# Stretches of the edge softmax shifted by half a stretch in a four-layer graph network

## The chip, the cores and the metric

The kernel runs on one core of one Trainium2 chip. A core has five engines with a queue of instructions each: TensorE (PE; its loads of weights are listed apart, as PEld), VectorE (DVE), ScalarE (ACT), GpSimd (POOL) and SyncE (SP), which here only issues DMAs. The metric is the device time of one execution in microseconds (us). The time before is 3351.46 us, the median of three runs (3344.36 to 3361.28).

## The reference, cut to what matters

A graph has 3125 nodes with 256 values each and 50000 edges, sorted by their target `dst`. Four layers follow one another, each as `x = layernorm(x + layer(x))`. Layer 0 is a gated message passing layer and layer 3 a relational one (a weighted sum over incoming edges, then block-diagonal products); the change touches neither. Layers 1 and 2 both need a softmax over the incoming edges of every node, for each head:

```python
# layer 1: 4 heads, 8 relations, 4 node types
score = sum(q_att[etype, dst] * k[src], axis=-1) * (relation_pri[etype] / sqrt(64))
m     = segment_max(score, dst)
ex    = exp(score - m[dst])
agg   = segment_sum(ex / segment_sum(ex, dst)[dst] * msg[etype, src], dst)
# layer 2: 8 heads of 64
e     = s_src[src] + s_tgt[dst];  e = where(e >= 0, e, 0.2 * e)
ex    = exp(e - segment_max(e, dst)[dst])
out   = elu(segment_sum(h[src] * ex / segment_sum(ex, dst)[dst], dst) @ Wo + bo)
```

All of it is float32; the edges are drawn so that some nodes have very many incoming edges (`dst` is 3125 times the square of a uniform number).

## The kernel before, in words

**Tiles, groups, stretches.** Nodes are kept in 25 tiles of 128. Edges are put into 416 *slot tiles* (`TT`) of 128 places each; a slot tile belongs to one node tile, so that sums over its edges are one matmul with a one-hot matrix (place to node). Four slot tiles are a *group* (`G`), of which there are 104, and sixteen are a *stretch* (`S`), of which there are 26. All this is worked out on the chip from `dst` during the set-up (`bucket`, line 213). A part of it, `segments` (line 360), makes for every slot tile five rows of 128 numbers, `seg`, which say where a node's run of edges starts and ends (0 or a large negative number `NEG`), and for the whole list three rows of one number per slot tile, `astart`, `aend` and `anew` (does a run reach from one tile into the next), from which `rows` is made, one row of two times sixteen per stretch. `seg` is stored by SyncE at line 403, the three rows are copied by VectorE at line 405, `rows` is put together at lines 407 to 410 and stored at 411.

**The softmax layers.** Layer 1 (line 1105) and layer 2 (line 1374) both call `edge_softmax` (line 714) with a function `score` of their own. `score` works on one group: GpSimd gathers the group's 512 rows from a table in memory with four indirect DMAs (line 509; a row is 2 KB in layer 1 and a little over that in layer 2), into one of seven buffers; SyncE loads the group's one-hots, two groups at a time (`onehots_back`, line 541; the DMA is at line 548); and then

- in layer 1 (line 1228) PE selects the targets' vectors (`pqe`, line 1237), VectorE multiplies them with the gathered rows (`pd`, line 1242) and sums over each head (`sc`, line 1243);
- in layer 2 (line 1390) PE selects the targets' scores (`pst`, line 1398) and three small VectorE instructions add the gathered ones and apply the slope (`pl`, `sc`, lines 1403 to 1405).

After the four groups of a stretch comes `softmax` (line 607) for its sixteen slot tiles at once. It is one chain that goes to and fro between engines: SyncE loads the stretch's rows of `seg` (line 615) and `rows` (line 619); PE transposes the scores so that each (head, tile) pair is a row (line 624); VectorE adds the mask (`smA`, line 627), runs a maximum scan forward and one backward along the row (`smf`, `smb`, lines 629 and 631); PE moves the last elements of the rows to one partition (lines 633, 634); VectorE and ScalarE scan over the sixteen tiles there and hand a running maximum on to the next stretch (`hand`, `smo`, lines 638 to 652); the result goes back (`cc`, line 649), VectorE takes it in (`smb`, line 660), subtracts (`smA`, line 661), PE transposes back (line 664) and ScalarE takes the exponential (`ex`, line 666). If the stretch isn't the first, the maximum of the node whose run goes on from the stretch before may have grown; then the sums of that node tile so far are multiplied with a factor (`dif` line 669, `fac` line 676, product at line 679).

`weigh` (line 682) then takes one group of an earlier stretch: ScalarE makes the one-hots float32 (line 693); VectorE multiplies some heads of the gathered rows with `ex` (line 697) and ScalarE the others (lines 694 and 701), which gives `r`; for every slot tile PE multiplies the one-hot with `r` (line 706) and VectorE adds the product to the node tile's sums in `acc` (line 711). A gather buffer is free for the next group when `r` is made.

**The order.** `edge_softmax` goes through the stretches. In each it scores group n of this stretch and then weighs group n of the stretch before, for the first three groups; the fourth group of the stretch before is weighed step by step between the steps of the softmax of this one. So the first stretch has nothing to weigh, and after the last one its four groups are weighed alone. Once the sums are whole, the layer divides by the summed weights (`rd`, line 1263 in layer 1, line 1419 in layer 2). With seven buffers the gathers of seven groups may be under way before the first group is weighed.

At the end of layer 1 the node tiles' outputs are turned into layer 2's table (`nodes2`, line 1316, and its weights' work at lines 1336 and 1337). Layer 2 needs its input x back in order of nodes: `x_back` (line 1357, the DMAs in `back`, line 1371) is kept on a list and issued from `edge_softmax` (line 726) when its third iteration begins. In what order the instructions stand in an engine's queue is set by the scheduler of the language's tile framework, from the order of the program and what each instruction needs; it may differ from the order of the program's text.

## Time and profile before

One execution under the profiler is shown; its time is 3366.77 us, its span 3365.0 us.

| what | before |
|---|---|
| median of three runs | 3351.46 us (3344.36 to 3361.28) |
| the profiled execution: time, span | 3366.77 us, 3365.0 us |
| mean granted clock of TensorE | 0.845 of full speed |
| PE, its weight loads, VectorE, ScalarE, GpSimd busy | 80, 52, 67, 43, 54% of the span |
| DMA | 658.40 MB, 196 GB/s over the span |
| layer 1, from the first `smA` (line 627) to `rd` (line 1263) | 1197.66 to 1811.01: 613.4 us |
| layer 2, from the first `smA` to `rd` (line 1419) | 1994.48 to 2672.97: 678.5 us |

How it is read: a busy share is that of an engine over the whole span; the page also gives it in 40 slices of 84.1 us each, as a digit of tenths. A line of the timeline has the start of an instruction in us from the span's start, its duration, its engine, its line in the kernel, the operation, what it writes and what it reads, with partitions x elements, and in brackets how long the engine was idle before it and what ended that. SPq and POOLq are the queues that issue DMAs.

### The profile page before, as it was taken

What the parts mean: (1) busy time and instruction counts of PE and PEld (TensorE: products, weight loads), DVE (VectorE), ACT (ScalarE), POOL (GpSimd) and SP (SyncE); (2) the same over time, 40 slices, a digit from 0 to 9 for tenths busy, and PEclk for the clock granted to TensorE, in tenths of its full rate; (3) what the DMA queues carried; (4) which work ended last, traced back from release to release, by engine and by line L of the source; (5) the groups of instructions that cost most, each with busy time, mean ns of one, the idle gap of its engine ahead of it and who ended that gap; (6) DMA issues with size and microseconds to landing.
All of it is one profiled execution on the core that took longest, in us unless ns stands there. A gap on an engine that the chain in (4) does not pass through costs nothing. (4 is left out here: it accounts for less than half of the span.)

```text
span 3365.0 us, 50575 instructions
## 1 busy us (share of the span) xinstructions
PE 2690.9 (80%) x12679; PEld 1750.5 (52%) x12679; DVE 2267.3 (67%) x6030; ACT 1460.9 (43%) x4405; POOL 1832.7 (54%) x1850
## 2 busy tenths in 40 slices
PE   2779999999979767777775847888888886888885
PEld 1357777775546345555553525666666664333333
DVE  2546676667655479888886437888888873555555
ACT  1427777774456334545543215656656553000001
POOL 3037777771044166666661556766766202777773
PEclk9889999999989878888887968888888886656566
DMA  7249998894067877777774367877877235333333
GB/s 164 74 134 296 298 289 290 288 287 141 32 248 285 313 224 241 231 235 233 231 232 132 123 209 200 227 226 223 228 223 225 78 125 221 106 106 105 105 106 92
DMA packets 240632, 658.40 MB, mean 196 GB/s; under 512 B 47976, under 2 KB 87028, under 8 KB 234029
## 3 DMA queue, kind: packets, MB, share of 16 engines
q0 software_dynamic: 132400, 484.37, 46.9%
q1 hardware_dynamic: 104278, 167.53, 15.2%
q10 hardware_dynamic: 3676, 3.23, 0.5%
q8 instruction: 122, 2.00, 0.2%
q14 instruction: 156, 1.28, 0.1%
HBM read 513.06 MB, written 151.58 MB: 198 GB/s over the span
## 5 line engine op out<-in xcount | busy, mean ns | idle before, releaser
L509 POOL DMA_INDIRECT gb<-table,s_src x832 | 859.1, 1033 | 371.6 <-issue 201.2
L706 PE MATMUL pr<-r,oh 128*128 128x260 f32 x2496 | 735.8, 441 | 82.2 <-DVE acc L711 32.6
L706 PEld LDWEIGHTS pr<-r,oh 128*128 128x128 f32 x2496 | 503.2, 217 | 219.5 <-issue 37.2
L1509 POOL DMA_INDIRECT ring<-table,b_rel x391 | 369.7, 946 | 317.9 <-DVE oh L1519 199.1
L701 ACT ACTIVATE r<-gb,ex 128x64 f32<-128x64 f32 x2080 | 522.3, 335 | 0.0
L509 POOL DMA_INDIRECT gb<-table,s_rel x416 | 404.4, 972 | 205.8 <-issue 110.0
L711 DVE TENSOR_TENSOR acc<-acc,pr 128x260 f32 (+1 forms) x832 | 457.9, 550 | 73.0 <-PE pr L706 59.4
L1538 PE MATMUL pa<-ring,oh 128*128 x832 | 420.5, 617 | 92.3 <-DMA ring<-table,b_rel 44.6
L1538 PEld LDWEIGHTS pa<-ring,oh 128*128 128x128 f32 x832 | 190.7, 278 | 322.4 <-DVE oh L1519 210.8
L1545 DVE TENSOR_TENSOR x<-x,pa 128x256 f32 x416 | 175.2, 421 | 227.8 <-PE pa L1538 225.6
L1237 PE MATMUL pqe<-q_all,oht 128*128 x1248 | 207.1, 304 | 94.6 <-DVE pd L1242 78.7
L693 ACT CAST oh<-ohb 128x512 f32<-128x512 bf16 x208 | 128.3, 618 | 314.2 <-PE pr L706 284.3
L589 ACT ACTIVATE r<-mv,eps 128x4 f32<-128x4 f32 (+2 forms) x31 | 9.1, 295 | 527.8 <-DVE mv L575 524.4
L697 DVE TENSOR_TENSOR r<-gb,ex 128x512 f32<-128x512 f32 (+1 forms) x208 | 225.7, 1086 | 13.3 <-ACT ex L666 9.0
L979 PE MATMUL pa<-gb,ohw 128*128 128x272 f32 x832 | 223.4, 402 | 4.5 <-DVE acc L981 2.9
L1237 PEld LDWEIGHTS <-oht 128*128 128x128 bf16 x1248 | 130.6, 106 | 128.4 <-issue 87.6
L961 PE MATMUL pre<-xb,oht 128*128 x1248 | 193.7, 273 | 0.0
L981 DVE TENSOR_TENSOR acc<-acc,pa 128x272 f32 x416 | 179.7, 432 | 5.1 <-PE pa L979 2.8
L928 DVE TENSOR_TENSOR places<-iota,s_dl 128x512 bf16<-128x512 f32 x104 | 71.9, 691 | 160.8 <-ACT ohw L976 160.8
L956 PE MATMUL pre<-gb,idb 128*128 128x512 bf16 x624 | 169.3, 380 | 5.3 <-DMA gb<-table,s_src 5.3
L967 DVE SCALAR_TENSOR_TENSOR hg<-hg,aw 128x256 f32<-128x256 f32 x416 | 159.3, 420 | 16.4 <-ACT hg L965 16.4
L979 PEld LDWEIGHTS pa<-gb,ohw 128*128 128x128 f32 x832 | 141.2, 190 | 54.6 <-issue 34.0
(383 smaller groups left out, 4302.0 us busy)
## 6 DMA issues: line engine op xcount, KB each, us to landing
ohb<-oh_d SPq DMA_DIRECT2D x104, 256.0 KB
oht<-oht_d SPq DMA_DIRECT2D x104, 256.0 KB
table<-row SPq DMA_DIRECT2D x25, 1024.0 KB
gb<-table,s_src POOLq DMA_INDIRECT x832, 4.5
oh_d<-places SPq DMA_DIRECT2D x52, 256.0 KB
oht_d<-oht SPq DMA_DIRECT2D x52, 256.0 KB
sgm<-seg SPq DMA_DIRECT2D x26, 320.0 KB
gb<-table,s_rel POOLq DMA_INDIRECT x416, 4.7
```

The source lines that it names most:

```text
L509: self.nc.gpsimd.indirect_dma_start(out=out, out_offset=None, in_=table, in_offset=bass.IndirectOffsetOnAxis(ap=idx[:, t:t + 1], axis=0))
L697: nc.vector.tensor_mul(r[:, :, :nd, :hw], v[:, :, :nd, :], ex[:, :nd, s0:s0 + G].rearrange("p h t -> p t h")[:, :, :, None].to_broadcast([ ...
L701: nc.scalar.activation(r[:, j, h, :hw], v[:, j, h, :], AF.Copy, scale=ex[:, h, s0 + j:s0 + j + 1])
L706: nc.tensor.matmul(pr[:, n, :HB * F], oh[:, j, :], r[:, j, n * HB:(n + 1) * HB, :].rearrange("p h f -> p (h f)"), start=True, stop=True)
L711: self.used(nc.vector, nc.vector.tensor_add(a, a, pr[:, :, :HB * F]))
L961: last = nc.tensor.matmul(q, oht[:, 0, j, :], xbr[:, ds(node * (3 * D) + n * D, D)], start=False, stop=False)
L979: nc.tensor.matmul(pa, ohw[:, j, :], gb[:, j, 0:ET + D], start=True, stop=True)
L981: self.used(nc.vector, nc.vector.tensor_add(a, a, pa))
L1237: last = nc.tensor.matmul(pq[:, j, :], oht[:, j, :], q_all[:, ds(node * (3 * D) + n * D, D)], start=n == 0, stop=n == 2)
L1509: st = nc.gpsimd.indirect_dma_start(out=ring[:, at:at + D], out_offset=None, in_=table, in_offset=bass.IndirectOffsetOnAxis(ap=b_rel[:, b: ...
L1538: last = nc.tensor.matmul(pa, oh[:, j, :], ring[:, ds(at, D)], start=True, stop=True)
L1545: self.used(nc.vector, nc.vector.tensor_add(a, a, pa))
```

## The change

The slot tiles keep their order and their groups. What moves is where a stretch begins: all stretches are shifted by eight slot tiles (half a stretch, `L = S // 2`). There are 27 instead of 26. The first holds eight empty places and then the groups g0 and g1; the 25 after it hold four groups each; the last holds the groups g102 and g103 and eight empty places. For an empty place no group is scored, gathered or weighed. Its scores are set to 0 (a `memset` of `sc` in the first and the last stretch), its rows of `seg` are filled so that it is masked, and `astart`, `aend`, `anew` and `rows` are longer by sixteen places. The softmax of the two short stretches has the same instructions with the same shapes as the others.

```diff
         self.s_dl = c.tile([P, TT], F32, name="s_dl")
         self.s_ty = self.early.tile([P, TT], F32, name="s_ty")
         self.s_w = c.tile([P, TT], F32, name="s_w")
-        NS = TT // S
+        NS = TT // S + 1
         self.NB = -(-E // P)
...
-        self.seg = self.dram.tile([TT, 5, P], F32, name="seg")
+        self.seg = self.dram.tile([TT + S, 5, P], F32, name="seg")
         self.rows = self.dram.tile([NS, 2, S], F32, name="rows")
-        self.astart, self.aend, self.anew = (c.tile([1, TT], F32, name=n) for n in ("astart", "aend", "anew"))
+        self.astart, self.aend, self.anew = (c.tile([1, TT + S], F32, name=n) for n in ("astart", "aend", "anew"))
         self.tnode = c.tile([1, TT], I32, name="tnode")
         with tc.tile_pool(name="bk", bufs=1, side="right") as b:
...
     def segments(self, w, bd, nxt, prv, bdf, sel, kd):
         tc, nc, TT = self.tc, self.nc, self.TT
-        C = bd.shape[1]
+        C, L = bd.shape[1], S // 2
         flag = w.tile([P, 2, C, P], F32, name="flag")
         nc.vector.tensor_tensor(flag[:, 0], prv, bd, op=ALU.not_equal)
         nc.vector.tensor_tensor(flag[:, 1], nxt, bd, op=ALU.not_equal)
...
                 nc.vector.tensor_add(edge[:M], sg[:M, 0, 0:1], sg[:M, 1, 0:1])
                 for n, col in enumerate((sg[:M, 3, P - 1:P], sg[:M, 4, 0:1], edge[:M])):
                     nc.tensor.matmul(rows[:, n, m0:m0 + M], col, self.ident[:M, :M], start=True, stop=True)
-                nc.sync.dma_start(self.seg[m0:m0 + M], sg[:M])
+                M0 = M
+                if m0 + M == TT:
+                    assert M % 32 == 0 and M < P
+                    nc.vector.memset(sg[M:M + L, 0], NEG)
+                    nc.vector.memset(sg[M:M + L, 1:], 0.0)
+                    nc.sync.dma_start(self.seg[0:L], sg[M:M + L])
+                    M0 = M + L
+                nc.sync.dma_start(self.seg[L + m0:L + m0 + M0], sg[:M0])
             for n, row in enumerate((self.astart, self.aend, self.anew)):
-                nc.vector.tensor_copy(row, rows[:, n, :TT])
-            rrow = w.tile([1, TT // S, 2, S], F32, name="rrow")
+                nc.vector.memset(row, NEG if n == 2 else 0.0)
+                nc.vector.tensor_copy(row[:, L:L + TT], rows[:, n, :TT])
+            rrow = w.tile([1, TT // S + 1, 2, S], F32, name="rrow")
             nc.vector.memset(rrow, NEG)
             st, en = (r.rearrange("p (s t) -> p s t", t=S) for r in (self.astart, self.aend))
             nc.vector.tensor_copy(rrow[:, :, 0, 1:], st[:, :, :S - 1])
...
         nc = self.nc
-        R = H * S
+        R, p0 = H * S, t0 + S // 2
         sg = w.tile([R, 5, P], F32, name="sgm")
-        nc.sync.dma_start(sg, bass.AP(tensor=self.seg.tensor, offset=self.seg.offset + t0 * 5 * P,
+        nc.sync.dma_start(sg, bass.AP(tensor=self.seg.tensor, offset=self.seg.offset + p0 * 5 * P,
                                       ap=[[0, H], [5 * P, S], [1, 5 * P]]))
-        s_of = t0 // S
+        s_of = p0 // S
         rr = w.tile([1, 2, H, S], F32, name="rr")
         nc.sync.dma_start(rr, bass.AP(tensor=self.rows.tensor, offset=self.rows.offset + s_of * 2 * S,
                                       ap=[[0, 1], [S, 2], [0, H], [1, S]]))
...
         ends = sm.tile([1, 2, H], F32, name="ends")
         nc.vector.scalar_tensor_tensor(hand[(s_of + 1) % 2][:, 0, :, 0], o[:, 0, :, S - 1],
-                                       self.astart[:, t0 + S - 1:t0 + S], outf[:, :, S - 1],
+                                       self.astart[:, p0 + S - 1:p0 + S], outf[:, :, S - 1],
                                        op0=ALU.add, op1=ALU.max)
         if s_of:
-            nc.vector.scalar_tensor_tensor(ends[:, 1], o[:, 1, :, 0], self.aend[:, t0:t0 + 1], outb[:, :, 0],
+            nc.vector.scalar_tensor_tensor(ends[:, 1], o[:, 1, :, 0], self.aend[:, p0:p0 + 1], outb[:, :, 0],
                                            op0=ALU.add, op1=ALU.max)
         yield
         for n in range(2):
...
         nc.scalar.activation(ex, eT.rearrange("p (h t) -> p h t", h=H), AF.Exp)
         if s_of:
             dif = sm.tile([1, H], F32, name="dif")
-            nc.vector.scalar_tensor_tensor(dif, ends[:, 1], self.anew[:, t0:t0 + 1], o[:, 0, :, 0],
+            nc.vector.scalar_tensor_tensor(dif, ends[:, 1], self.anew[:, p0:p0 + 1], o[:, 0, :, 0],
                                            op0=ALU.add, op1=ALU.max)
             nc.vector.tensor_sub(dif, o[:, 0, :, 0], dif)
             at = sm.tile([1, P], F32, name="at")
...
         F = hw + 1
         HB = 4
         r = w.tile([P, G, H, F], F32, name="r")
-        s0 = t0 % S
+        s0 = (t0 + S // 2) % S
         oh = w.tile([P, G, P], F32, name="oh")
         nc.scalar.copy(oh, ohb)
         nc.scalar.copy(r[:, :, :, hw], ex[:, :, s0:s0 + G].rearrange("p h t -> p t h"))
...
                 pass
         nc = self.nc
-        before, ex = [], None
-        for t0 in range(0, self.TT + S, S):
-            last = t0 == self.TT
-            if t0 == 2 * S:
+        before, ex, L = [], None, S // 2
+        for t0 in range(-L, self.TT + L + S, S):
+            last = t0 == self.TT + L
+            if t0 == 2 * S - L:
                 with self.tc.issue_after(self.uses[nc.vector.engine][-1]):
                     while self.later:
                         self.later.pop()()
             held = []
             if not last:
                 sc = sm.tile([P, H, S], F32, name="sc")
+                if t0 < 0 or t0 + S > self.TT:
+                    nc.vector.memset(sc, 0.0)
             for n in range(S // G):
+                g0 = t0 + n * G
                 if not last:
-                    held.append(score(t0 + n * G, sc[:, :, n * G:(n + 1) * G]))
-                if before and (last or n < S // G - 1):
+                    held.append(score(g0, sc[:, :, n * G:(n + 1) * G]) if 0 <= g0 < self.TT else None)
+                if before and before[n] and (last or n < S // G - 1):
                     value, oh = before[n]
-                    done(self.weigh(w, ps, acc, oh, ex, value, H, t0 - S + n * G, on_act))
+                    done(self.weigh(w, ps, acc, oh, ex, value, H, g0 - S, on_act))
             if last:
                 break
             rest = iter(())
-            if before:
+            if before and before[-1]:
                 value, oh = before[-1]
                 rest = self.weigh(w, ps, acc, oh, ex, value, H, t0 - G, on_act)
             got = None
```

In the changed kernel the lines of `softmax` stand 9 further down, and those of the layers 12.

## The prediction

> **What bounds the kernel now.** I read the page first: span and busy shares.
>
> ```profile
> span 3365.0 us, 50575 instructions
> ...
> DVE  2546676667655479888886437888888873555555
> ...
> L697 DVE TENSOR_TENSOR r<-gb,ex 128x512 f32<-128x512 f32 (+1 forms) x208 | 225.7, 1086 | 13.3 <-ACT ex L666 9.0
> ```
>
> Line two is VectorE's busy share in 40 slices: the change lives in the two softmax layers, slices 15 to 21 (layer 1) and 25 to 32 (layer 2), where VectorE is at 7 to 9 tenths. The third is the product of gathered rows with the softmax weights, once per group of four slot tiles. Then the table by stage, for the middle of both layers (columns: stretch of time, its length, busy time of PE, its weight loads, VectorE, ScalarE, GpSimd, granted clock, DMA share, GB/s):
>
> ```profile
> core 0: us, PE busy (x) PEld busy (x) DVE busy (x) ACT busy (x) POOL busy (x), PEclk, DMA share, GB/s
> 1245.00:1785.00 540.00, 411.74 (x2114) 286.40 (x2115) 478.38 (x997) 266.25 (x1022) 356.63 (x367) 0.86 0.76 234
> 2036.00:2640.00 604.00, 495.67 (x2191) 370.33 (x2190) 510.79 (x1121) 366.77 (x1430) 406.56 (x377) 0.88 0.78 220
> ```
>
> VectorE is busy 478 of 540 us and 511 of 604; PE 76 and 82%. VectorE, with PE close behind, sets the pace, so a softmax chain that is added inside has a price, and one that falls where VectorE idles has none. Next the times at which each stretch's softmax starts (smA, line 627), in the timeline; first layer 1, then layer 2, and last in each the first use of the finished sums (rd):
>
> ```profile
> 1197.66 0.28 DVE L627 TENSOR_TENSOR smA<-mis,sgm 64x128 f32<-64x128 f32 x1 [1.12 <-PE mis L624]
> ...
> 1226.19 0.28 DVE L627 TENSOR_TENSOR smA<-mis,sgm 64x128 f32<-64x128 f32 x1 [0.58 <-PE mis L624]
> ...
> 1249.96 0.27 DVE L627 TENSOR_TENSOR smA<-mis,sgm 64x128 f32<-64x128 f32 x1
> ...
> 1784.76 0.27 DVE L627 TENSOR_TENSOR smA<-mis,sgm 64x128 f32<-64x128 f32 x1
> ...
> 1811.01 0.24 DVE L1263 TENSOR_SCALAR rd<-acc 128x100 f32<-128x100 f32 x1
> ```
>
> ```profile
> 1994.48 0.29 DVE L627 TENSOR_TENSOR smA<-mis,sgm 128x128 f32<-128x128 f32 x1 [0.57 <-PE mis L624]
> ...
> 2036.29 0.29 DVE L627 TENSOR_TENSOR smA<-mis,sgm 128x128 f32<-128x128 f32 x1 [0.67 <-PE mis L624]
> ...
> 2060.70 0.27 DVE L627 TENSOR_TENSOR smA<-mis,sgm 128x128 f32<-128x128 f32 x1
> ...
> 2641.62 0.28 DVE L627 TENSOR_TENSOR smA<-mis,sgm 128x128 f32<-128x128 f32 x1
> ...
> 2672.97 0.34 DVE L1419 TENSOR_SCALAR rd<-acc 128x200 f32<-128x200 f32 x1
> ```
>
> From the 3rd softmax to the 26th is 534.8 us in layer 1, 23 stretches of 23.25, and 580.9 us in layer 2, 23 of 25.26. Before and after them are a head and a tail. What the head of layer 1 waits for (GpSimd's gathers, and the product pd that consumes them):
>
> ```profile
> 1208.62 1.22 DVE L1242 TENSOR_TENSOR pd<-gb,pqe 128x1024 f32<-128x1024 f32 x1 [1.29 <-DMA gb<-table,s_rel]
> ...
> 1213.89 0.95 POOL L509 DMA_INDIRECT gb<-table,s_rel  x1 [8.07 <-ACT r L701]
> ...
> 1222.06 1.22 DVE L1242 TENSOR_TENSOR pd<-gb,pqe 128x1024 f32<-128x1024 f32 x1 [2.77 <-DMA gb<-table,s_rel]
> ```
>
> All 28 gathers that seven buffers allow are issued by 1205.8; the 29th waits 8.07 us for ScalarE, which needs the first softmax's result (ex, 1211.2). So pd of the eighth group starts only at 1222.06. The head of layer 2 (SyncE's queue, PE, GpSimd):
>
> ```profile
> 1973.48 20.09 SPq L1371 DMA_DIRECT2D x<-own  x5
> ...
> 2002.73 9.56 SPq L548 DMA_DIRECT2D oht<-oht_d  x2
> ...
> 2009.18 0.55 PE L1398 MATMUL pst<-s_tgt,oht 128*128 x4 [14.74 <-DMA oht<-oht_d]
> ...
> 2020.01 1.47 POOL L509 DMA_INDIRECT gb<-table,s_src  x1 [16.53 <-ACT r L694]
> ...
> 2022.10 8.45 PE L706 MATMUL pr<-r,oh 128*128 128x260 f32 x28
> ```
>
> SyncE spends 20 us issuing the reload of x; the third pair of one-hots stands behind it, PE stands 14.7 us for that, and the first weighted sum (line 706) starts at 2022.10.
>
> **The change, part by part.** I number groups g0 to g103. The built order of the changed kernel's instructions shows where each part lies.
>
> *Setup.* Five small memsets, one more store, rows 16 longer. The three of the rows move to VectorE's start; the two of the 32-row tile (bounded by rrow's, 0.75 us) lie in the 3.27 us in which VectorE waits for PE at 205.2 to 208.5; the added store is 0.32 us on SyncE, ahead of the rows store at 213.31, which waits for VectorE. Four memsets of score tiles (two a layer) lie where VectorE waits: for the first gather, or inside a chain. Cost 0 to 1, taken 0.2 us. If the wait at 205 were gone, the memsets would cost their 1 us.
>
> *Middle.* On VectorE the order from the 3rd softmax to the 26th is the same, instruction by instruction, in both layers; each layer has as many gathers, scores, sums and loads of one-hots there. 0 us. The extra chain is thus in head and tail alone.
>
> *Head of layer 1.* The first softmax now comes after g1, not g3. g1's score ends at 1187.4 (pd at 1185.01, then 1.22+1.22), so smA is at 1188, and the chain runs while VectorE waits for g2 (1188.64), g3 (1194.06) and g5 (1204.04): ex is there by 1202, not 1211.2. g0's product follows pd of g5 at 1205.3, its buffer is free at 1206.1, and the 29th gather has no 8 us to wait. The second softmax comes after g5's score, at 1208.5 (before: after g7's, 1226.19); a stretch like the second of before (23.8 us) leads to the third: 1232.3, 17.7 earlier. It must be earlier for having two groups fewer ahead of it: two pitches of 4.73 (pd at 1373.61, 1378.38, 1383.07), 9.5 us. That is the upper bound (no gain from the filled wait); with a stretch of 21.8, the shorter kind, it is 19.7. I take 17.7, since every step has its row.
>
> *Tail of layer 1.* Before: 26.25 us from the 26th smA to rd. Now two more scores, two more weighted groups and the 27th chain stand there too. To the 27th smA 13.5 us: chain 26 (5.1, 1759.73 to 1764.83), two pd and two reductions (1.13 each, by their pitch), three products (0.6), five sums (0.34), one rescale. Then its chain among eleven sums, 9.5 (1386.93 to 1394.07, 7.1 with six sums; five more and one product). Then two weighted groups, half of the 17.8 us that four took from ex at 1793.2 to rd: 9. Of the weights' work for the next layer (L1336 and its reduction, 0.6 us each), which stood wholly before rd, half moves behind it, where 1.2 us are in the way. Together 33.2: +7.0. Bounds: chain wholly hidden 29 (+2.8), nothing hidden 38 (+11.8). Layer 1: -17.7+7.0 = -10.7.
>
> *Head of layer 2.* The stall until 2009.2 stays: the reload of x keeps its place on SyncE. But the chain of the first softmax is through before it, up to its second half. ex comes at 2012.2 instead of 2016.03, g0's buffer is free at 2015.6 instead of 2020.01. One-hot pair five now stands behind a row load and a segment load that wait for VectorE; issued at 2011.8, landing 5.2 us later as the pair issued at 2015.84 did, it lets PE start the weighted sums at 2017.1, 5 us earlier; what is queued behind it on SyncE is the next one-hots alone. The second softmax starts at 2016.5; one stretch of 25.3 and 1.5 us of waiting lead to the third: 2043.3, 17.4 earlier. Bounds: 9.8 (two pitches of 4.9) and 19.7.
>
> *Tail of layer 2.* Before 31.35. Now 20.5 from the 26th smA to the 27th (11.3 to its rescale as at 2616.31 to 2627.57, then two groups), and then 21 sums, 5.25 groups at the 4.75 us of the last four before (2653.14 to 2672.1), and 2.5 us of PE for the chain: 48. +16.6; bounds 43 and 52 (+11.7, +20.7). Layer 2: -17.4+16.6 = -0.8.
>
> *Moved past queues.* Each layer issues a 27th segment and row load on SyncE (0.6 us each); SyncE is idle between one-hots in the middle. GpSimd issues the same gathers. The reload of x is still the third iteration's, same place.
>
> The chain itself, by rows: VectorE 4.2 us in layer 1 (17 instructions, 0.14 to 0.43 each), 4.9 in layer 2, and it does not shrink with eight empty tiles. This is in the heads and tails above. The Trainium skill's "Perfetto Trace Analysis", section "Optimizing Scalar/DVE Operations", speaks against the change: each VectorE instruction has about 60 ns of fixed overhead, and larger operations are to be grouped. By that rule alone, as an estimate, 2x17 more instructions would cost 2 us, and the sum would be plus 2. The 1x4 rows at 0.20 us agree that size hardly matters here; the heads' idle time decides.
>
> **Sum.** 0.2-10.7-0.8 = -11.3 us. Against the profiled execution (3366.77; span 3365.0 and 1.8 around it) 3355.5; it lies 15 above the median, so the forecast is 3340 against 3351.46. About 0.5%, 17 us, is what a measurement of this kernel tells from no change (its three runs spread over 17). I forecast no measurable change, on the faster side.
>
> **Rivals.**
> - *The heads gain all and the tails hide the 27th chain.* For it: PE and ScalarE wait on VectorE in the old tails, and the sums around the chain fill it. Against it: PE's own 4.75 us per group in layer 2. Heads 19.7 and 19.7, tails +2.8 and +11.7: -25, 3327.
> - *The early softmax gains nothing.* If g2 to g6 arrive late or one-hot pair five holds PE as long as before, the heads give only 9.5 and 9.8, and the tails stay: 0.2-9.5+7.0-9.8+16.6 = +4.5, 3356. Against it: the landings of g2 to g6 do not depend on the softmax.
> - *Slower: layer 1 loses its short stretches.* Its stretches alternate between 21.8 and 24.6 us, by whether pd stands before the wait for the rescale's factor. If the shift puts gathers late against that pd, the 11 short ones become long, 11x2.8 = +31, net +19.5: 3371. It decides when more than (17+11.3)/2.8 = 10 of the 11 turn. For it: pd waits for gathers 6.1 us in this stage, so there is little slack. Against it: the order is the same.
>
> **How the numbers follow.** Forecast 0.62, of which 0.04 passes 17 us; first rival 0.21 (faster); second 0.09; third 0.08 (slower), and 0.02 of the second, with both tails at their upper bounds too (+13.4 and more), is slower. Faster 0.25, same 0.65, slower 0.10. Range: 3325 (the first rival and 2 us) to 3359 (the second and 3).
>
> **What would show it.** The 3rd smA comes 17 to 18 us earlier after each layer's first score than before; GpSimd's 8.07 us wait is gone, the 16.5 one is near 12; 23 stretches still take 535 and 581 us; from the 26th smA to rd is 33 and 48 us, with a 27th inside. I am wrong if the middle's pace moves by over 0.5 us a stretch, or if the extra chain stalls VectorE in the tails by its full length.

## The result, and the profile after

Over 20 runs of each on one chip the changed kernel takes 3367.99 us (median; 3362.92 to 3377.47) and the kernel before 3359.84 (3344.36 to 3367.34): ratio 1.003, 95% interval 1.0019 to 1.004, so 6 to 13 us slower. That is under the 0.5% that the forecast called no change, but it lies on the other side of zero: the forecast was 11.3 us faster. The three runs shown before had a low median; the 20 put the base 8.4 us higher. The forecast range, 3325 to 3359, reached from 26 us faster to 8 slower than its base; the change came out slower than its base by 8 us (medians) to 10 (ratio).

The page of the changed kernel (span, and VectorE's busy share in 40 slices) looks like that of before:

```profile
span 3368.1 us, 50689 instructions
...
DVE  2547766666655388888885547888888773555555
```

So the place is not to be seen on the page, and the stages have to be measured. The table by stage for the 23 stretches from the 3rd smA to the 26th (columns as before) shows that the middle is the same: 409.8 us of PE and 473.8 of VectorE in 534 us of layer 1, at the same clock and the same GB/s.

```profile
core 0: us, PE busy (x) PEld busy (x) DVE busy (x) ACT busy (x) POOL busy (x), PEclk, DMA share, GB/s
1231.00:1765.00 534.00, 409.77 (x2118) 285.82 (x2117) 473.76 (x990) 263.46 (x1013) 359.28 (x371) 0.86 0.75 234
2050.00:2630.00 580.00, 477.70 (x2113) 357.50 (x2111) 492.04 (x1079) 353.99 (x1380) 394.76 (x364) 0.87 0.78 221
```

The times of smA (line 636 now) in the timeline of VectorE, layer 1: the first three, the 26th, the 27th, and rd.

```profile
1185.85 0.28 DVE L636 TENSOR_TENSOR smA<-mis,sgm 64x128 f32<-64x128 f32 x1 [0.52 <-PE mis L633]
...
1207.12 0.28 DVE L636 TENSOR_TENSOR smA<-mis,sgm 64x128 f32<-64x128 f32 x1 [0.58 <-PE mis L633]
...
1231.11 0.28 DVE L636 TENSOR_TENSOR smA<-mis,sgm 64x128 f32<-64x128 f32 x1
...
1765.08 0.28 DVE L636 TENSOR_TENSOR smA<-mis,sgm 64x128 f32<-64x128 f32 x1
...
1784.64 0.28 DVE L636 TENSOR_TENSOR smA<-mis,sgm 64x128 f32<-64x128 f32 x1
...
1802.65 0.24 DVE L1275 TENSOR_SCALAR rd<-acc 128x100 f32<-128x100 f32 x1
```

The same of layer 2:

```profile
1982.81 0.29 DVE L636 TENSOR_TENSOR smA<-mis,sgm 128x128 f32<-128x128 f32 x1 [0.57 <-PE mis L633]
...
2013.24 0.28 DVE L636 TENSOR_TENSOR smA<-mis,sgm 128x128 f32<-128x128 f32 x1
...
2050.20 0.29 DVE L636 TENSOR_TENSOR smA<-mis,sgm 128x128 f32<-128x128 f32 x1 [0.46 <-PE mis L633]
...
2629.82 0.28 DVE L636 TENSOR_TENSOR smA<-mis,sgm 128x128 f32<-128x128 f32 x1
...
2650.13 0.28 DVE L636 TENSOR_TENSOR smA<-mis,sgm 128x128 f32<-128x128 f32 x1
...
2677.74 0.34 DVE L1431 TENSOR_SCALAR rd<-acc 128x200 f32<-128x200 f32 x1
```

From these times, with each layer's first score (pd at 1179.41, pl at 1978.22), the whole difference can be laid out by stage. The column for before has two profiled executions: the one shown (first score at 1181.75 and 1982.19) and a second from the experiments, on a chip of the same speed. The two differ by 14 us in span and by up to 6 in a stage, and the changed kernel has one profile here, so a row of 1 or 2 us says nothing.

| stage | before, two profiles | after | measured change (against their mean) | predicted |
|---|---|---|---|---|
| start to the first pd of layer 1 | 1181.8, 1177.6 | 1179.4 | -0.3 | +0.2 |
| head of layer 1: first pd to 3rd smA | 68.2, 66.0 | 51.7 | -15.4 | -17.7 |
| middle: 3rd to 26th smA | 534.8, 533.5 | 534.0 | -0.2 | 0 |
| tail: 26th smA to rd | 26.2, 24.3 | 37.6 | +12.3 | +7.0 |
| rd to the first pl of layer 2 | 171.2, 171.8 | 175.6 | +4.1 | 0 |
| head of layer 2: first pl to 3rd smA | 78.5, 78.5 | 72.0 | -6.5 | -17.4 |
| middle | 580.9, 575.4 | 579.6 | +1.5 | 0 |
| tail | 31.3, 30.7 | 47.9 | +16.9 | +16.6 |
| rd to the end | 692.0, 692.9 | 690.4 | -2.1 | 0 |

The sum is +10.3 against the mean span of the two (3357.85). That the ratio of the 20 runs says the same is in part luck, with spans that far apart. Three rows differ from the forecast by more than 3 us: layer 1's tail, what follows it, and layer 2's head.

**Layer 1's head** did what was forecast. GpSimd's wait of 8.07 us for the first softmax is gone; its timeline has 1.95 us there (put down to issue and not to ScalarE), and later 4.44:

```profile
1204.53 0.94 POOL L518 DMA_INDIRECT gb<-table,s_rel  x1 [1.95 <-issue]
...
1219.05 0.94 POOL L518 DMA_INDIRECT gb<-table,s_rel  x1 [4.44 <-ACT r L710]
```

**Layer 1's tail.** VectorE's timeline inside the 26th softmax, ScalarE's at the same time, and the sigmoid of before:

```profile
1767.95 0.27 DVE L651 TENSOR_TENSOR_SCAN smo<-rr,hand 1x64 f32<-1x64 f32 x1
...
1772.40 0.28 DVE L654 TENSOR_TENSOR_SCAN smo<-rr,hand 1x64 f32<-1x64 f32 x1 [4.18 <-ACT hand L648]
```

```profile
1765.30 1.28 ACT L1268 ACT_TABLE_LOAD   x1 [2.50 <-PE mis L633]
...
1771.56 0.20 ACT L1268 ACTIVATE sk<-sk 128x4 f32<-128x4 f32 x1 [4.97 <-DMA sk<-in_L_gnn_skip]
...
1772.18 0.19 ACT L648 COPY hand<-mis 1x60 f32<-1x60 f32 x1
```

```profile
1781.52 0.20 ACT L1256 ACTIVATE sk<-sk 128x4 f32<-128x4 f32 x1 [3.88 <-DMA sk<-in_L_gnn_skip]
```

On its way from smA to ex the chain passes ScalarE in two small copies (hand, line 648, and cc, line 658). In ScalarE's queue the sigmoid of the skip weights and the load of its function table (1.28 us; both line 1268) stand ahead of the first copy, and the sigmoid waits 4.97 us for its DMA. VectorE stands 4.18 us for it with the chain in its hands. Before, the sigmoid waited for its DMA too, but between two softmaxes (table and sigmoid 1776.35 to 1781.72 on ScalarE; the 26th smA was at 1784.76).

**Layer 2's head.** From the first pl to the second smA the forecast was 34.3 us, the trace has 35.0. Then the third smA comes 37.0 us later, where 25.3 + 1.5 were forecast. VectorE, PE and GpSimd before it, and ScalarE's end of the second softmax:

```profile
2040.02 0.19 DVE L1416 TENSOR_TENSOR pl<-pl,gb 128x32 f32<-128x32 f32 x1 [1.10 <-DMA gb<-table,s_src]
...
2046.86 0.19 DVE L1416 TENSOR_TENSOR pl<-pl,gb 128x32 f32<-128x32 f32 x1 [5.76 <-DMA gb<-table,s_src]
...
2050.20 0.29 DVE L636 TENSOR_TENSOR smA<-mis,sgm 128x128 f32<-128x128 f32 x1 [0.46 <-PE mis L633]
```

```profile
2005.44 0.55 PE L1410 MATMUL pst<-s_tgt,oht 128*128 x4 [16.51 <-DMA oht<-oht_d]
...
2047.88 2.07 PE L715 MATMUL pr<-r,oh 128*128 128x260 f32 x4 [5.63 <-DVE acc L720]
...
2049.74 0.42 PE L633 MATMUL mis<-ident,sc 128*128 128x128 f32 x1
```

```profile
2012.66 1.48 POOL L518 DMA_INDIRECT gb<-table,s_src  x1 [13.13 <-ACT r L710]
...
2031.79 0.94 POOL L518 DMA_INDIRECT gb<-table,s_src  x1 [8.90 <-DVE r L706]
...
2041.61 0.94 POOL L518 DMA_INDIRECT gb<-table,s_src  x1 [0.30 <-DMA gb<-table,s_src]
```

```profile
2027.98 0.28 ACT L675 ACTIVATE ex<-mis 128x128 f32<-128x128 f32 x1 [1.71 <-PE mis L673]
```

The same in the kernel before: the score of g11, which is the last one ahead of its third smA, and the end of its second softmax.

```profile
2057.68 0.19 DVE L1404 TENSOR_TENSOR pl<-pl,gb 128x32 f32<-128x32 f32 x1 [1.86 <-DMA gb<-table,s_src]
```

```profile
2044.73 0.28 ACT L666 ACTIVATE ex<-mis 128x128 f32<-128x128 f32 x1 [1.21 <-PE mis L664]
```

The pl at 2046.86 is the score of g10. It belongs to the fourth stretch, but it was built into VectorE's queue ahead of sums that the third smA waits for, through PE (its 5.63 us wait, then the transpose at 2049.74). Its four gathers stand behind those of g9, which waited 8.90 us for a buffer that the second softmax frees; the last of g10's was issued at 2041.61. So VectorE stood 5.76 us with the third softmax behind it. Before, only the last group of the third stretch itself (g11) waited there, 1.86 us. And the second softmax took 14.7 us from smA (2013.24) to ex (2027.98), where it took 8.4 before (2036.29 to 2044.73).

### The profile page after: what moved, and what is told of

It reads as the page before. It is cut to its first block, busy times and chain, and to the rows that moved or that the text cites. A ratio compares the mean times of both kernels' runs of the same rounds, so it can differ in the third digit from the quotient of the medians.

```text
span 3368.1 us, 50689 instructions
## 1 busy us (share of the span) xinstructions
PE 2702.5 (80%) x12703; PEld 1760.6 (52%) x12703; DVE 2275.5 (68%) x6069; ACT 1462.4 (43%) x4413; POOL 1828.4 (54%) x1850
## 3 DMA queue, kind: packets, MB, share of 16 engines
q14 instruction: 156, 1.28, 0.1%
## 5 line engine op out<-in xcount | busy, mean ns | idle before, releaser
L715 PEld LDWEIGHTS pr<-r,oh 128*128 128x128 f32 x2496 | 505.7, 218 | 222.7 <-issue 38.4
L1550 PE MATMUL pa<-ring,oh 128*128 x832 | 425.9, 624 | 87.1 <-DMA ring<-table,b_rel 51.4
```

What stands on the lines that cost most here:

```text
L715: nc.tensor.matmul(pr[:, n, :HB * F], oh[:, j, :], r[:, j, n * HB:(n + 1) * HB, :].rearrange("p h f -> p (h f)"), start=True, stop=True)
L1550: last = nc.tensor.matmul(pa, oh[:, j, :], ring[:, ds(at, D)], start=True, stop=True)
```

## The experiments

Two theories, and rivals as they came up. **A**: the loss is in particular waits, VectorE's for g10 in layer 2's head and ScalarE's for the skip weights in layer 1's tail. **B**: an extra softmax chain costs some 5 us in each tail, wherever it is put. The runs fell on several chips. On one the kernel before takes 3360 us, as in the comparison; on the four others 3954 to 4042. In the profiles that are used here, layer 2's middle took 575 to 583 us on the first and 634 to 712 on the others. There the intervals of the times are 12 to 18 us to either side, so a change of 5 us is read from the stages, not from the times.

### The score of g10, the chain, and both (fast chip)

The kernel before once more is the base; it took 3360.54 us, ratio 1.0002 (0.9988 to 1.0016).

> The kernel before, for its stages beside those of the others on the same chip. Both theories: the same time as before; from the first pl of layer 2 to the third smA some 80 us, from the 26th smA of layer 1 to rd 26 us, of layer 2 31 us.

Its stages are the second column above. Then the score of g10 was put behind the third smA:

```diff
-        nc.vector.tensor_add(A, sT, sg[:, 0, :])
+        self.smA_in = nc.vector.tensor_add(A, sT, sg[:, 0, :]).ins
...
-                    nc.vector.tensor_reduce(pl, pst.rearrange("p j n h -> p j h n"), axis=AX.X, op=ALU.add)
+                    with self.tc.issue_after(self.smA_in) if g0 // G in (10,) else nullcontext():
+                        nc.vector.tensor_reduce(pl, pst.rearrange("p j n h -> p j h n"), axis=AX.X, op=ALU.add)
```

> The changed kernel; in layer 2 the score of g10 is built behind smA of the third softmax, to which it doesn't belong, and no longer ahead of it. Theory D (VectorE stands 5.8 us for the gather of g10 with the third smA behind it): the third smA comes 30 to 32 us after the second in place of 37, and 5 to 6 us earlier after the first pl; the wait for g10 is then inside the third softmax or gone, and half of the gain or more is kept at the fourth smA. Rival F (the third stretch is bound by the sums of g2 to g4): 35 us or more.

It took 3360.77 us, ratio 1.0003 (0.9992 to 1.0014) against before: the 10 us are gone but for 1. (The changed kernel itself did not run beside it; the next one, which gains nothing and did, took 8 us longer.) In VectorE's timeline (second smA, the score of g9, third and fourth smA) the third comes 30.7 us after the second, and the fourth keeps the gain (24.5 later):

```profile
2007.03 0.28 DVE L636 TENSOR_TENSOR smA<-mis,sgm 128x128 f32<-128x128 f32 x1
...
2034.05 0.19 DVE L1417 TENSOR_TENSOR pl<-pl,gb 128x32 f32<-128x32 f32 x1 [1.15 <-DMA gb<-table,s_src]
...
2037.70 0.28 DVE L636 TENSOR_TENSOR smA<-mis,sgm 128x128 f32<-128x128 f32 x1
...
2062.24 0.27 DVE L636 TENSOR_TENSOR smA<-mis,sgm 128x128 f32<-128x128 f32 x1
```

From the first pl to the third smA it is 65.2 us, 6.8 less than in the changed kernel. So 6.8 of the 10.9 us by which layer 2's head missed its forecast are one group's score in the wrong place of VectorE's queue. It is a matter of order, and of three small instructions: no work was taken away.

The rest of that miss, the second softmax's 14.7 us, was laid to the 32 products of g0 and g1 that stand beside it on PE. In the next kernel the sums of g0 are built behind the softmax's first step:

```diff
-                if before and before[n] and (last or n < S // G - 1):
+                second = t0 == S - L and H == 8
+                if before and before[n] and (last or n < S // G - 1) and not second:
...
                 rest = self.weigh(w, ps, acc, oh, ex, value, H, t0 - G, on_act)
+                if second:
+                    value, oh = before[-2]
+                    rest = chain(self.weigh(w, ps, acc, oh, ex, value, H, t0 - 2 * G, on_act), rest)
```

> The changed kernel; in layer 2's second stretch alone, the sums of g0 are built behind the first step of the second softmax, not ahead of it, so that on PE the softmax's matmuls stand before all but three of the 32 products of g0 and g1. Theory D (the second softmax takes 14.7 us from smA to ex, against 8.5 before, because those products stand ahead of it on PE): it falls to 8 to 10 us, and the third smA comes 4 to 6 us earlier after the first pl than in the changed kernel. Rival E (PE's half clock makes the chain slow): it stays at 12 or more.

3369.07 us, 1.0031 (1.0016 to 1.0046): no gain. The third smA came 70.4 us after the first pl (72.0 in the changed kernel), and the second softmax took 15.5 us. VectorE's timeline (smA, a sum, smb), and PE's ahead of the first product:

```profile
2015.12 0.28 DVE L637 TENSOR_TENSOR smA<-mis,sgm 128x128 f32<-128x128 f32 x1
...
2020.53 0.70 DVE L721 TENSOR_TENSOR acc<-acc,pr 128x520 f32 x1 [3.38 <-PE pr L716]
...
2021.14 0.42 DVE L641 TENSOR_TENSOR_SCAN smb<-sgm,smf 128x128 f32<-128x128 f32 x1
```

```profile
2017.90 0.58 PE L1415 MATMUL pst<-s_tgt,oht 128*128 x4 [4.08 <-DMA oht<-oht_d]
```

The backward scan now stands behind the first sum, and that waits 3.38 us for the first product, which itself stands behind a score's matmul that waits for one-hots. And the edit did not do on PE what was expected of it: in its trace all 32 products still run between the second smA and the softmax's last transpose (line 674), as they do in the changed kernel. So this run is no test of theory D. Other kernels have rows that bear on it. With the shift of 12 and of 4 (below) one group and three groups stand there in place of two, 16 and 48 products, and the second softmax took 10.7 and 16.0 us, at a mean granted clock of 0.74 and 0.86; in the changed kernel it was 0.79. Rival E, PE's clock, has rows too: in the kernel before the third and the fourth softmax of layer 2 both had 24 products beside them and took 11.1 us at a clock of 0.81 and 9.5 at 1.00, and the second, with about 20, took its 8.4 at 1.00. The table by stage of the changed kernel has a granted clock of 0.50 up to 2014 and 0.62 in the seven us after. So both fit, but no run changed the products or the clock alone. Why this softmax takes 15 us and not 8.4 stays open between them.

```profile
core 0: us, PE busy (x) PEld busy (x) DVE busy (x) ACT busy (x) POOL busy (x), PEclk, DMA share, GB/s
1990.00:2005.00 15.00, 0.00 (x0) 0.08 (x1) 0.17 (x1) 0.43 (x1) 7.40 (x8) 0.50 0.97 348
...
2014.00:2021.00 7.00, 7.00 (x24) 5.14 (x23) 3.45 (x8) 0.76 (x3) 5.17 (x7) 0.62 0.68 187
2021.00:2030.00 9.00, 6.03 (x34) 4.55 (x32) 7.28 (x22) 3.33 (x14) 1.58 (x2) 0.98 0.59 172
```

Last, both moves of layer 2, and the skip weights of layer 1 loaded at the layer's start:

```diff
             acc = wp.tile([P, NT * H * F], F32, name="acc1")
+            sk = wp.tile([P, T], F32, name="sk")
+            nc.scalar.dma_start(sk, brow(skip, T))
+            nc.scalar.activation(sk, sk, AF.Sigmoid)
...
-                sk = st.tile([P, T], F32, name="sk")
-                nc.scalar.dma_start(sk, brow(skip, T))
-                nc.scalar.activation(sk, sk, AF.Sigmoid)
```

> The two moves of layer 2 and the early skip weights of layer 1 together. Theory D: 10 us from layer 2's head and 4 from layer 1's tail, 12 to 14 faster than the changed kernel, so about level with before or up to 5 faster where the changed kernel is 10 slower.

3358.2 us, 0.9994 (0.9982 to 1.0005): level with before, 10 us faster than the changed kernel by the medians, and 2.6 faster than the kernel with the late score of g10 alone, which the intervals do not tell apart. The 26th smA, the 27th and rd of layer 1:

```profile
1767.13 0.28 DVE L637 TENSOR_TENSOR smA<-mis,sgm 64x128 f32<-64x128 f32 x1
...
1783.58 0.28 DVE L637 TENSOR_TENSOR smA<-mis,sgm 64x128 f32<-64x128 f32 x1
...
1800.41 0.24 DVE L1280 TENSOR_SCALAR rd<-acc 128x100 f32<-128x100 f32 x1
```

That is 33.3 us, against 37.6, 38.1 and 37.3 in the three kernels with the late skip weights. Over the profiles of all kernels with layer 1 shifted by eight it is 37.0 to 38.5 us in the eight with late skip weights and 33.3 to 34.7 in the five with early ones.

### The skip weights, the buffers and the reload, one by one (slower chip)

> The changed kernel once more, as the base for the three that follow. Theory A and rival B: +8 to +12 against before where a stretch of layer 1 takes 23 us; more where gathers land later and a stretch takes 30, since a gather that waits for a buffer then costs more.

The changed kernel took 3969.73 us there, 1.0014 (0.9981 to 1.0048). The skip weights alone, by the last diff:

> The changed kernel with the load of the skip weights and their sigmoid moved from behind layer 1's loop to its start (the same work, earlier). Theory A: VectorE's 4.2 us wait for ScalarE inside the 26th chain of layer 1 goes, and the tail of layer 1 (26th smA to rd) falls from 37.6 to about 33: 4 us faster than the changed kernel. Rival B (the tail is long because of the chain alone): 0 to 1.

3961.42 us, 0.9976 (0.9944 to 1.0008); layer 1's tail 34.1 us, with the late skip weights 37.0. That is some 3 us in the tail; theory A had about 4, and the times cannot tell it from the rival's 0 to 1. Eight gather buffers:

```diff
-            with tc.tile_pool(name="e2g", bufs=7) as gp, tc.tile_pool(name="e2", bufs=2) as w, \
+            with tc.tile_pool(name="e2g", bufs=8) as gp, tc.tile_pool(name="e2", bufs=2) as w, \
...
-        o = sm.tile([1, 2, H, S], F32, name="smo")
+        o = sm.tile([1, 2, H, S], F32, name="smo", bufs=1)
...
-            at = sm.tile([1, P], F32, name="at")
+            at = sm.tile([1, P], F32, name="at", bufs=2)
```

> The changed kernel with eight gather buffers in layer 2 in place of seven (room for it from one buffer for smo and two for at in place of three). Theory A: the gather of g9 no longer waits for the second softmax; the third smA of layer 2 comes about 31 us after the second, not 37: 6 us faster than the changed kernel, more if the middle gains too. Rival C (the long stretch is PE at half its clock alone): the third smA stays 36 to 37 us after the second.

The third smA came 31.2 us after the second (36.6 with seven), as theory A had it, but the second came 4.5 us later after the first, and the fourth 38.4 after the third (26.4 with seven). To the fourth smA it was 108.3 us from the first pl against 96.7: the wait moved by one stretch and nothing was kept there. (The edit also takes buffers from smo and at, and what that costs was not tested.) 3958.65 us, 0.9978 (0.9946 to 1.0011), does not tell it from the changed kernel. The reload of x:

```diff
-            if t0 == 2 * S - L:
-                with self.tc.issue_after(self.uses[nc.vector.engine][-1]):
-                    while self.later:
-                        self.later.pop()()
+            if t0 >= 4 * S and self.later:
+                with self.tc.issue_after(self.seg_in):
+                    self.later.pop(0)()
...
-                self.later.append(x_back)
+                self.later += [part(a, 2) for a in range(0, NT - 1, 2)] + [part(NT - 1, 1)]
```

> The changed kernel with the reload of x cut into 13 pieces, one behind each stretch's segment load from the fourth stretch on, so that SyncE is free at the head of layer 2. Theory A: PE's 16.5 us wait for the third pair of one-hots goes, the third smA of layer 2 comes 20 us earlier after the first pl (52 in place of 72), and the pieces cost nothing in the middle: 20 us faster than the changed kernel, 10 faster than before. Rival C (the head is bound by GpSimd's gathers, which need 50 us for ten groups whatever SyncE does): 5 us or less.

3978.66 us, 1.0027 (0.9997 to 1.0058): not faster. From the first pl to the third smA 69.8 us, with the reload in front 70.3. SyncE no longer spends 17 to 20 us on x at that point, but it does not go on earlier for that. Two issues of one-hots that follow each other in its queue, and VectorE at the time of the second:

```profile
2407.09 0.33 SPq L557 DMA_DIRECT2D oht<-oht_d  x1
```

```profile
2425.95 0.32 SPq L557 DMA_DIRECT2D oht<-oht_d  x1
2425.96 0.26 DVE L1424 TENSOR_REDUCE pl<-pst 128x32 f32<-128x96 f32 x1 [10.23 <-remote]
```

Between the two, SyncE issues nothing for 18.5 us. VectorE, which has stood for 10.23 us, goes on at the same moment, and for what ended its wait the profile names no engine and no DMA of this core. So the reload is not what sets the length of this head. Rival C, as the next three runs put it, has it that the DMA engines are full of the 28 gathers and whatever is asked for there lands late: while PE stands, the changed kernel's DMA engines are at a share of 0.97 with 348 GB/s (the row 1990 to 2005 above). In the stall of the kernel with the late reload (2414 to 2426) the share is 0.75 with 215 GB/s, so full engines are not the whole of it.

### Taking the one-hots' buffers away as a cause (another slower chip)

Four buffers for the one-hots of layer 2, the late reload, and the early skip weights, in three kernels:

```diff
-                t = p.tile([P, 2 * G, P], BF, name=name)
+                t = p.tile([P, 2 * G, P], BF, name=name, bufs=self.pairs[name])
...
+            self.pairs = {'ohb': 4, 'oht': 4}
```

> The kernel before with layer 2's one-hot pairs in four buffers in place of two, the reload of x in 13 pieces from the fourth stretch on, and the early skip weights. Theory G (the third pair of one-hots waits for a buffer and behind the reload of x): PE's 14.7 us wait at the head of layer 2 goes, the third smA comes 60 us after the first pl in place of 78: 15 to 20 us faster than before. Rival C (the DMA engines are full with 28 gathers, and whatever comes later lands later): 75 us, and less than 5 faster.

> The changed kernel with the same three edits and the score of g10 behind the third smA. Theory G: the third smA comes 48 to 55 us after the first pl; 20 to 25 us faster than the changed kernel, and against the kernel before with the same edits between -3 and +5, since the tails keep their extra chain. Rival C: 62 us or more, 12 faster than the changed kernel.

> Shifted in layer 1 alone, with the early skip weights, the four buffers for one-hots and the late reload of x. Theory A (layer 1's shift gains some 4 us once ScalarE no longer holds its 26th chain, layer 2's gains nothing): 2 to 6 us faster than the kernel before with the same edits. Rival B (an extra chain costs as much in layer 1): 2 to 6 slower than it.

Times: 3966.45 (0.9965, 0.9934 to 0.9996), 3979.83 (1.0014, 0.9984 to 1.0043) and 3976.15 us (0.9989, 0.9955 to 1.0023). In the second, which also has the late score of g10, the head of layer 2 took 62.8 us, about what that move alone leaves (65.2 on the fast chip); but its fourth smA came 44.0 us after the third, so the gain was not kept there as it was on the fast chip (24.5). In the third, which has layer 2 unshifted, it took 85.7 us, and 86.4 in the kernel without the freed head that ran beside it. So theory G falls in these two: neither the reload nor the number of one-hot buffers sets the length of this head. SyncE's queue is not cleared by that, for in both traces it still issues nothing for 17.8 and 19.4 us between two one-hots, and what it waits for the profile does not name. For the kernel before, with the same three edits, the interval lies 2 to 26 us below before; its profiled execution took 27 us longer than its median, so its stages are not used, and it was run once.

### One layer at a time, and other sizes

One layer shifted, the other not; the set-up makes the unshifted `rows` as well:

```diff
+            rrow0 = w.tile([1, TT // S, 2, S], F32, name="rrow0")
...
-        s_of = p0 // S
+        s_of = (t0 + self.L) // S
+        rows = self.rows if self.L else self.rows0
...
-        before, ex, L = [], None, S // 2
+        before, ex, L = [], None, self.L
```

> Stretches shifted in layer 1 alone (layer 2 takes the rows of the unshifted stretches, which the set-up makes as well). Theory A, from the two traces: within layer 1 the shift is worth -6 us (623.2 against 629.3 us from the first pd to rd), and the stretch behind it gives up to 4 of that back; so 2 us faster than before, between -6 and +2. Rival B (the 10 us come from an extra softmax chain in each layer's tail, alike in both layers): +5.

> Stretches shifted in layer 2 alone. Theory A: the loss lies here, +9 us against before (699.5 against 690.8 us from the first pl to rd), and the third softmax again comes some 37 us after the second. Rival B: +5, half of the whole.

And the shift by 4 and by 12 slot tiles, with `L` at 4 or 12 throughout:

> The shift is 4 slot tiles in place of 8: the first stretch holds g0 to g2, the last g103 alone. Still 27 softmaxes a layer. Theory A (the second softmax's chain meets a cold PE and only as many free buffers as the first stretch had groups): three buffers come free at once, so the head of layer 2 loses less and the whole is 0 to +5 against before. Rival B (the extra chain costs its 5 us in each tail, whatever the shift): +10 as with 8.

> The shift is 12 slot tiles: the first stretch holds g0 alone, the last g101 to g103. Theory A: one buffer comes free, the head gains no more than with 8 while the tail grows by another group of 4.7 us in each layer: +14 to +22 against before. Rival B: +10.

Against before (3954.19 us) the four took 3953.04 (1.0005, 0.9972 to 1.0038), 3983.49 (1.008, 1.0051 to 1.011), 4001.11 (1.0118, 1.0076 to 1.016) and 4002.83 us (1.0123, 1.0078 to 1.0167). The stages of the four, all on one chip; the rows for 0 and 8 come from the kernels with one layer shifted:

| shift | layer 1 head + tail | layer 2 head + tail |
|---|---|---|
| 0 | 99.8 + 25.9 = 125.7 | 81.4 + 30.7 = 112.1 |
| 4 | 81.6 + 28.3 = 109.9 | 78.8 + 44.2 = 123.0 |
| 8 | 77.4 + 37.1 = 114.5 | 71.4 + 47.7 = 119.1 |
| 12 | 73.4 + 46.2 = 119.6 | 64.5 + 51.4 = 115.9 |

In both layers a larger shift makes the head shorter and the tail longer, but not by the same: from 4 to 8 to 12 each further group takes some 4 us from layer 1's head and adds 9 to its tail, and takes 7 from layer 2's head and adds 3.6 to its tail. In layer 2 the sum is 4 to 11 us above the unshifted one of this chip, on the fast chip 10 (119.9 against 109.9 and 109.2). These are single profiles; on the slower chips the unshifted sum of layer 2 itself ranges from 111.8 to 117.9 us over four of them, so the differences between the sizes may be chance. In layer 1 the sum is below the unshifted one, because the unshifted head is long on this chip (99.8, where the fast chip has 66 to 68). By time, layer 2 shifted alone is 20 to 43 us slower than before and layer 1 alone is level with it; heads and tails hold 7 of those us. Theory A's guess that a larger shift costs more, and rival B's flat +10, are both off: the times of the last two are 47 and 49 us up, and heads and tails hold none of that. Most of it lies in the middles, which on this chip ranged from 656.7 (layer 1 shifted alone) to 706.1 us (shift 4) in layer 2; what moves them there was not found.

Layer 1 alone was run twice more, the second time also with the early skip weights:

> Shifted in layer 1 alone, as in the first run, which fell on a chip where before takes 3954 us. Theory A: -4 to +2 us against before where before takes 3360; the rest of the changed kernel's 8 to 10 us is layer 2's. Rival B: +4 to +6, half of the whole.

> Shifted in layer 1 alone. Theory A by the stage times on the chip where before takes 3360 us: head -15, tail +12, the work between the layers +3, sum 0: within 4 us of before. On the chip where before takes 3960 us: head -22, tail +11, between +4: -7, 0.998.

> The same with the early skip weights: the 26th chain of layer 1 no longer waits for ScalarE, 4 us less than the run before; -4 against before where before takes 3360 us (0.999), -11 where it takes 3960 (0.997).

All on slower chips: 3962.63 (0.9952, 0.9922 to 0.9981), 4047.88 (1.0003, 0.9968 to 1.0038) and 4039.37 us (1.0, 0.9964 to 1.0035). Three runs of one kernel at 1.0005, 0.9952 and 1.0003 say that it makes little difference, and not of which sign. Two of the 18 runs have an interval below before, the second of these three (its repetitions do not) and the kernel before with the freed head, run once; so none is shown to beat before.

## Why the prediction was wrong, step by step

- **Setup, middle:** right. Start -0.3, middles -0.2 and +1.5 us; the middle's pace did not move.
- **Head of layer 1, -17.7:** right, -15.4; the chain fills VectorE's waits, and the 29th gather waits 1.95 us in place of 8.07.
- **Tail of layer 1, +7.0:** mis-sized, +12.3. The step was "To the 27th smA 13.5 us": it took 19.6. Its 5.1 us for chain 26 are rows of another chain of layer 1 (1759.73 to 1764.83, the 25th of before), in which ScalarE's copy came at once; here the same rows took 9.2 us, with the 4.18 us of waiting behind the sigmoid of the skip weights. With the early skip weights the tail is 33.3 us, but that this is the forecast's 33.2 is luck: to the 27th smA it is still 16.5 us (forecast 13.5), and from there to rd 16.8 (forecast 19.7).
- **Between the layers, 0:** +4.1 in this profile, and 171.9, 175.5 and 176.1 us in three other kernels shifted in both layers (before 171.2 and 171.8). Some of it may be the weights' work that moved behind rd, which was named. It was not tested.
- **Head of layer 2, -17.4:** this step failed. "One stretch of 25.3 and 1.5 us of waiting lead to the third": 37.0. A stretch of the middle was put where the queues are those of a start: VectorE's 5.76 us wait for g10's gather ahead of the third smA, and the second softmax 14.7 us in place of 8.4. The step before it, the second smA 34.3 us after the first pl, was right (35.0). The forecast's lower bound of 9.8 us did not hold either, for it left no room for a new wait. The comparison of VectorE's order began at the third smA, and the misplaced score is just ahead of it. The move of that score gave back 6.8 us of the head and 7 to 9 of the time (by medians and by ratios); the other 4 us of this step, in the second softmax, stay open.
- **Tail of layer 2, +16.6:** right, +16.9, and right in its parts: 20.3 us to the 27th smA (forecast 20.5) and 27.6 from there (27.4).

Of the rivals, "the early softmax gains nothing" came nearest in number, +4.5, but not in cause: its condition did not come (layer 1's head gained 15.4, and layer 2's weighted sums began 3.6 us earlier, 5 by the forecast), and it has the tails as they were forecast. The rule of the Trainium skill that was weighed ("Perfetto Trace Analysis", section "Optimizing Scalar/DVE Operations", about 60 ns for a VectorE instruction on SBUF and about 125 on PSUM, of which the forecast took the first) gave, as an estimate, a sum of +2. The sign was the measured one, but the runs put the loss in waits and not in the count of instructions: the kernel that takes two of them away has all of the added instructions and is level with before.

## What to carry to other kernels

A shift of a pipeline by part of a period shortens its head, lengthens its tail and adds one round; here the middle gave nothing back, so the whole was decided by what each queue holds in the first rounds and the last. Price these from their own queues, all engines that the chain passes, and not from a round of the middle. A score that is scheduled one group early in an engine's queue can cost its whole wait (here 5.76 us); look for work of the next round ahead of the present one's critical step, and for late loads (here a few skip weights) in the queue of an engine that the chain only touches.

## What the runs showed of the hardware

Chips differ more than the changes studied. The kernel before takes 3360 us on one and 3954 to 4042 on the four others. Layer 1's middle shows it in the tables by stage: in 400 us the changed kernel on the fast chip did 306.4 us of PE work at 233 GB/s and a granted clock of 0.86,

```profile
core 0: us, PE busy (x) PEld busy (x) DVE busy (x) ACT busy (x) POOL busy (x), PEclk, DMA share, GB/s
1300.00:1700.00 400.00, 306.37 (x1582) 214.11 (x1582) 354.71 (x750) 195.81 (x754) 266.29 (x276) 0.86 0.74 233
```

and the kernel with layer 1 shifted alone, on a slower one, 257.6 us at 176 GB/s and 0.76:

```profile
core 0: us, PE busy (x) PEld busy (x) DVE busy (x) ACT busy (x) POOL busy (x), PEclk, DMA share, GB/s
1700.00:2100.00 400.00, 257.55 (x1195) 175.42 (x1193) 268.53 (x557) 148.15 (x572) 198.16 (x206) 0.76 0.59 176
```

A stretch of layer 1 takes 31 us there in place of 23. Tails and layer 2's head were nearly the same on both (tails 37.0 and 48.8 against 37.6 and 47.9, head 70.3 against 72.0 in the changed kernel), so these stages could be compared across chips where whole times could not. Layer 1's unshifted head could not (99.8 against 66 to 68). What makes a chip slower was not tested.
